# Cross-attention block on one NeuronCore: the first queries and scores in another order, matmuls on the identity ahead of them, the rotary table by a series, weights loaded in pieces

## The chip, the cores and the metric

The kernel runs on one NeuronCore of a Trainium2 chip. The engines named here are TensorE (PE: matmuls and weight loads), VectorE (DVE), ScalarE (ACT), GpSimd (POOL) and SyncE (SP, which issues nearly all DMA transfers). The metric is the device time of one execution in microseconds; the number given for a kernel is the median over its runs.

## The reference

The input is 64 sequences of 32 tokens, 256 wide, and a context of 257 rows of 128 for each sequence. Three residual stages follow each other, each on a layer norm of what stands so far:

1. Cross-attention with 16 heads of 64: queries from the tokens (weights Wq, 256 x 1024), keys and values from the context (Wk, Wv), softmax over 257 context rows, output projection Wo and bias.
2. Self-attention over the 32 tokens of a sequence with 4 heads of 64. Half of each head's width is rotated: `ang[pos, i] = pos * base**(-i/16) * 2*pi/31`, with `base = sigmoid(freq) * c1 + c2` and one input number `freq`; the rotation uses `cos(ang)` and `sin(ang)`.
3. A feed-forward stage with 8 experts, of which each token uses the 2 with the highest router scores.

All is float32.

## The kernel before, in words

Tokens are worked on in 16 tiles of 128 (four sequences each), in the function `block_kernel`. The work has three stretches: a start (constants, loads, the first queries and scores), a loop over 64 sequences in which cross-attention, self-attention and routing of several tiles are interleaved, and the experts' blocks after it.

**Order.** `manual_schedule` (L80) leaves SP and TensorE in the order in which the program writes them. DVE, ACT and POOL are ordered by a planner ahead of the run: it moves an instruction to where it expects the engine to be idle and the inputs to be there, so something written late can stand early in its queue. On the chip each queue is then worked off in that fixed order.

**Loads.** `load` (L98) issues a DMA on SP. In order: `base` (the input number freq, L129), token tiles 0 and 1 (L131), the queries' weights `xwq_sb` (1 MB, L132) and the keys' weights transposed, `xwk_sb` (0.5 MB, L133), the context of tile 0 (L134, two transfers of 0.5 MB), `xwv_sb`, `last_sb`, `xwo_sb`, token tiles 2 and 3 (L139), and the weights of the later stages. After them come eight transfers of zero rows to the DRAM buffer `routed` and one to `out` (L220, L222), from the tile `none`.

**Constants.** POOL makes the identity (L86), zeroes `diag`, `u_ring` and `p_last` (L167, L176, L179) and makes index tables (`iota`, L183).

**Queries.** `cross_queries(c)` (L305) is a generator for two token tiles. Its first step normalises them (`normed`: statistics on DVE, the power -1/2 on POOL at L242, the scaling on DVE at L245). The next transposes them (`transposed`, L248: four transposes on TensorE, two copies on ACT at L253). Then four projections of four heads each (L345, evacuated by ACT at L352) alternate with `of_heads` (L318), which multiplies by the keys' weights (L324) so that scores can be formed on the context itself; its two halves are evacuated by DVE (L337) and ACT (L335). Here `qh` has one buffer, and the PSUM tag `a`, from which `bank` (L231) takes, has three.

**Scores.** `cross_probs(t, b, ..)` (L359) is a generator of four steps for one sequence, each for four heads: scores (L369), maximum on DVE (L373), exp with sum on ACT (L374); after every second one the sums' reciprocal and the scaling on DVE (L379, L381). The scores have three PSUM buffers (tag `s`). `probs_transposed` (L389) and `cross_mix` (L399) use the result one sequence later.

**The start** (L883 to L930): the first step of `cross_queries(0)`; the rotary table, `cos` and `sin`, in the block at L886 to L924 (sigmoid and two sines on ACT, a power of 128 x 16 on POOL, small operations on DVE); all remaining steps of `cross_queries(0)`; the first step of `cross_queries(1)`; then all four steps of `cross_probs(0, 0)`.

**The loop** (L931): for each sequence n it transposes the probabilities, forms the scores of the next sequence, mixes, and takes steps of three generators, "near", "far" and "ahead", as the table `steps` (L875) says. "near" starts as `last_rows` (L259: products with the last context row, stored to DRAM; `load_last`, L296, brings rows of it back) and is `rest(t)` from then on (L597: cross output, self-attention, routing). The rotary table is first read in `self_attention` of tile 0 (L460), which the fifth step of `rest(0)` reaches, in sequence n = 7, the eighth.

Of the kernel before, what the change touches and what calls it, by code (L numbers as in the profile page):

```python
# [9 lines left out]
FP = mybir.dt.float32  # L10
# [40 lines left out]
def block_kernel(  # L51
# [36 lines left out]
    nc.gpsimd.memset(minus_half, -0.5)  # L88
    zero = const.tile([P, 1], FP, name="zero")
    nc.gpsimd.memset(zero, 0.0)  # L90
    half_pi = const.tile([P, 1], FP, name="half_pi")
    nc.gpsimd.memset(half_pi, math.pi / 2)
    expert_id = const.tile([P, NE], FP, name="expert_id")
    nc.gpsimd.iota(
        expert_id, [[1, NE]], base=0, channel_multiplier=0, allow_small_or_imprecise_dtypes=True
# [2 lines left out]
    def load(dst, src):  # L98
        nc.sync.dma_start(out=dst, in_=src)
# [26 lines left out]
        return kvT, kvA  # L126

    base = const.tile([P, 1], FP, name="base")
    load(base, freq.partition_broadcast(P))  # L129
    for t in range(2):  # L130
        load_tokens(t)  # L131
    load(xwq_sb, xwq.rearrange("(c p) k -> p c k", p=P))  # L132
    load(xwk_sb, xwk_t.rearrange("(c p) k -> p c k", p=P))  # L133
    context0 = load_context(0)  # L134
    load(xwv_sb, xwv)
    load(last_sb, ctx_last)
    load(xwo_sb, xwo.rearrange("(c p) k -> p c k", p=P))
    for t in range(2, 4):
        load_tokens(t)  # L139
    load(xbo_bc, xbo.partition_broadcast(P))  # L140

    awqkv_sb = const.tile([P, 2, 3 * D], FP, name="awqkv_sb")
# [18 lines left out]


    routed = tc.dram_tile([NE * CAP, RW], FP, name="routed")

    diag = [const.tile([P, AH, P], FP, name=f"diag{i}") for i in range(2)]
    for d in diag:
        nc.gpsimd.memset(d, 0.0)  # L167

    u_ring = [const.tile([P, D], FP, name=f"u{i}") for i in range(3)]
    p_last = [
        [const.tile([P, 32], FP, name=f"p_last{i}_{b}") for b in range(4)] for i in range(2)
    ]
    for u in u_ring:
        nc.gpsimd.memset(u, 0.0)  # L176
    for ring in p_last:
        for p in ring:
            nc.gpsimd.memset(p, 0.0)  # L179

    def iota(shape, pattern, base, by_partition, name):
        it = const.tile([P] + shape, FP, name=name)
        nc.gpsimd.iota(  # L183
            it,
            pattern,
            base=base,
            channel_multiplier=by_partition,
            allow_small_or_imprecise_dtypes=True,
        )
        return it  # L190

    ones = const.tile([P, P], FP, name="ones")
    nc.gpsimd.memset(ones, 1.0)

    before = iota([P], [[1, P]], 0, -1, "before")
    nc.vector.tensor_scalar(before, before, 0.0, None, ALU.is_gt)
    region = iota([1, NE], [[0, 1], [CAP, NE]], 0, 0, "region")
    expert_id2 = iota([2, NE], [[0, 2], [1, NE]], 0, 0, "expert_id2")

    upto = iota([NE, NE], [[1, NE], [-1, NE]], 0, 0, "upto")  # L200
    nc.vector.tensor_scalar(upto, upto, 0.0, None, ALU.is_ge)

    late = iota([LATE], [[1, LATE]], 0, 0, "late")
    in_lane = iota([LATE // LANES, LANES], [[1, LATE // LANES], [0, LANES]], FAR, 0, "in_lane")
    late_expert = iota([LATE, NE], [[0, LATE], [1, NE]], 0, 0, "late_expert")

    early = iota([EARLY // 2, 2], [[1, EARLY // 2], [EARLY // 2, 2]], 0, 0, "early")
    early_expert = iota([EARLY, NE], [[0, EARLY], [1, NE]], 0, 0, "early_expert")
    row = iota([1], [[0, 1]], 0, 1, "row")
    minus_spare = iota([1], [[0, 1]], -TOK, -1, "minus_spare")  # L210
    token = iota([NT], [[P, NT]], 0, 1, "token")

    seen = const.tile([P, NE], FP, name="seen")
    nc.gpsimd.memset(seen, 0.0)
    xp = pool("xp", 3)
    none = xp.tile([P, RW], FP, tag="xg", bufs=5, name="none")
    nc.gpsimd.memset(none, 0.0)

    for e in range(NE):
        load(routed[e * CAP : e * CAP + P, :], none)  # L220

    load(out[TOK : TOK + P, :], none[:, :D])  # L222

    qp = pool("q", 2)
    pp = pool("p", 2)
    ptp = pool("pt", 2)
    wk = pool("wk", 2)
    sm = pool("sm", 4)
    tb = pool("tb", 1)

    def bank(shape, name):  # L231
# [568 lines left out]
    def late_blocks(done):  # L800
# [67 lines left out]
        )  # L868
        return bl, total

# [12 lines left out]
    work = {"near": last_rows(), "far": iter(()), "ahead": cross_queries(0)}  # L883
    next(work["ahead"])

    with tc.tile_pool(name="rope", bufs=1) as rp:  # L886
        pos = rp.tile([P, 1], FP, name="pos")
        for s in range(P // SEQ):
            nc.gpsimd.iota(
                pos[s * SEQ : (s + 1) * SEQ, :],  # L890
                [[0, 1]],
                base=0,
                channel_multiplier=1,
                allow_small_or_imprecise_dtypes=True,
            )
        expo = rp.tile([P, 16], FP, name="expo")
        nc.gpsimd.iota(
            expo, [[-1, 16]], base=0, channel_multiplier=0, allow_small_or_imprecise_dtypes=True
        )
        expo16 = rp.tile([P, 16], FP, name="expo16")  # L900
        nc.vector.tensor_scalar(expo16, expo, 1.0 / 16.0, None, ALU.mult)
        sig = rp.tile([P, 1], FP, name="sig")
        nc.scalar.activation(sig, base, AF.Sigmoid, bias=zero)
        base2 = rp.tile([P, 1], FP, name="base2")
        nc.vector.tensor_scalar(base2, sig, SDT_L, MIN_L * BASE, ALU.mult, ALU.add)
        base16 = rp.tile([P, 16], FP, name="base16")
        nc.vector.tensor_copy(base16, base2.to_broadcast([P, 16]))
        inv_freq = rp.tile([P, 16], FP, name="inv_freq")
        nc.gpsimd.tensor_tensor(inv_freq, base16, expo16, ALU.pow)
        ang = rp.tile([P, 16], FP, name="ang")  # L910
        nc.vector.tensor_scalar(ang, inv_freq, pos, ANGLE, ALU.mult, ALU.mult)

        s4 = rp.tile([P, 16], FP, name="s4")
        c4 = rp.tile([P, 16], FP, name="c4")
        nc.scalar.activation(s4, ang, AF.Sin, bias=zero, scale=0.25)
        nc.scalar.activation(c4, ang, AF.Sin, bias=half_pi, scale=-0.25)
        s2 = rp.tile([P, 16], FP, name="s2")
        c2 = rp.tile([P, 16], FP, name="c2")
# [203 lines left out]
```

## Time and profile before

| what | value |
|---|---|
| median of 3 runs | 852.11 us (851.6 to 853.08) |
| the profiled execution | 853.89 us, its span 851.9 us |
| TensorE busy | 794.0 us (93% of the span) |
| DVE, ACT, POOL busy | 489.2, 382.3, 147.4 us |
| mean granted TensorE clock | 0.986 |
| DMA | 62.71 MB, mean 74 GB/s |

The span goes from the first to the last instruction of the profiled execution. In the lines shown below, a row of the timeline gives start and duration in microseconds, the engine, the line of the kernel, the operation, the tiles written and read, and in brackets how long the engine was idle before it and what ended this. A float32 matmul appears as two instructions, a transpose as one. L-numbers are lines of the kernel before.

### The profile page before, as it was taken

To read this page: it belongs to the slowest core of one execution; us is meant where nothing else is said; L and a number is where in the kernel's file an instruction comes from. 1 tells how busy PE (TensorE), PEld (TensorE's weight loads), DVE (VectorE), ACT (ScalarE), POOL (GpSimd) and SP (SyncE) were. 2 spreads that over 40 slices of the span, in tenths; PEclk is the share of its full clock that TensorE was granted. 3 is DMA by queue.
4 is the path that set the end of the run, shared out by engine and by line. 5 is a ranking of instruction groups with operands and counts; after the bars stand their busy time and mean duration, and the time that the engine had idled before them with its cause. 6 is when DMAs were issued, how large, how long until landed. Compare 5 with 4: busy or idle time off the path is not lost. (4 is left out here: it accounts for less than half of the span.)

```text
span 851.9 us, 15173 instructions
## 1 busy us (share of the span) xinstructions
PE 794.0 (93%) x5240; PEld 611.9 (72%) x5240; DVE 489.2 (57%) x2006; ACT 382.3 (45%) x1082; POOL 147.4 (17%) x209
## 2 busy tenths in 40 slices
PE   4899999999999999999999999999949999999994
PEld 3567677677767766776766777666647799999993
DVE  2456656766676676667676666767626733333331
ACT  2565545455455445546554545554414332222220
POOL 5001011111101011121101011110112422322222
PEclk9999999999999999999999999999979999999997
DMA  8421102020120202021120202012061297357321
GB/s 300 125 53 53 63 1 72 1 85 19 55 75 11 74 0 86 7 67 37 49 72 2 72 1 72 20 53 55 1 258 13 69 318 216 47 110 221 52 38 22
DMA packets 32031, 62.71 MB, mean 74 GB/s; under 512 B 5256, under 2 KB 22672, under 8 KB 30416
## 3 DMA queue, kind: packets, MB, share of 16 engines
q1 hardware_dynamic: 25424, 52.65, 19.0%
q0 software_dynamic: 6528, 9.06, 6.0%
q8 instruction: 43, 0.70, 0.3%
q14 instruction: 36, 0.29, 0.1%
HBM read 83.23 MB, written 13.16 MB: 113 GB/s over the span
## 5 line engine op out<-in xcount | busy, mean ns | idle before, releaser
L374 ACT ACTIVATE pr<-s,nmx 128x257 f32<-128x257 f32 x256 | 120.8, 479 | 72.6 <-DVE nmx L373 71.4
L369 PE MATMUL s<-kv,q 128*128 128x257 f32 x512 | 143.4, 389 | 7.6 <-ACT pr L374 7.6
L373 DVE TENSOR_REDUCE nmx<-s 128x1 f32<-128x257 f32 x256 | 103.8, 420 | 61.7 <-PE s L369 59.9
L402 PE MATMUL pa<-pt,kv 128*128 128x512 f32 x256 | 123.3, 604 | 5.0 <-ACT ov L426 5.0
L369 PEld LDWEIGHTS s<-kv,q 128*128 128x128 f32 x512 | 88.8, 192 | 25.1 <-ACT pr L374 12.2
L396 ACT COPY pt<-tp 128x512 f32<-128x512 f32 x128 | 75.9, 593 | 65.2 <-PE tp L392 65.1
L392 PEld LDWEIGHTS tp<-ident,pr 128*128 128x128 f32 x512 | 60.7, 144 | 33.7 <-issue 20.9
L392 PE MATMUL tp<-ident,pr 128*128 128x128 f32 x512 | 81.4, 280 | 1.2 <-DVE pr L381 1.1
L381 DVE TENSOR_SCALAR pr<-pr,inv 128x256 f32<-128x256 f32 x256 | 80.5, 357 | 2.9
L405 ACT COPY cT<-pa 128x512 f32<-128x512 f32 x64 | 37.5, 586 | 88.7 <-PE pa L402 88.7
L578 POOL DMA_INDIRECT routed<-xr,rslots x32 | 32.8, 1025 | 250.7 <-DVE pr L381 105.4
L402 PEld LDWEIGHTS pa<-pt,kv 128*128 128x128 f32 x256 | 44.9, 190 | 40.6 <-issue 29.1
L345 PE MATMUL pqh<-xqT,xwq_sb 128*128 128x256 f32 x256 | 62.5, 389 | 4.3 <-ACT xqT L253 4.3
L763 POOL DMA_INDIRECT out_x<-y_late,to_late x28 | 43.4, 1550 | 110.3 <-DVE gate_late L705 41.4
L435 PE MATMUL po<-xwo_sb,ov 128*128 128x256 f32 x256 | 61.9, 386 | 0.0
L345 PEld LDWEIGHTS pqh<-xqT,xwq_sb 128*128 128x128 f32 x256 | 48.6, 195 | 11.6 <-ACT xqT L253 4.7
L435 PEld LDWEIGHTS po<-xwo_sb,ov 128*128 128x128 f32 x256 | 49.7, 194 | 7.1
L379 DVE RECIPROCAL inv<-sums 128x2 f32<-128x2 f32 x128 | 20.6, 161 | 55.9 <-ACT pr L374 55.2
L745 DVE SCALAR_TENSOR_TENSOR g_late<-pb_late,lane,sa_late 128x128 f32<-128x128 f32 x72 | 20.3, 343 | 55.5 <-PE pb_late L726 37.0
L374 ACT ACTIVATION_READ_ACCUMULATOR pr<-s,nmx 128x1 f32 x256 | 51.8, 203 | 0.0
L410 POOL TENSOR_TENSOR xb<-x,xbo_bc 128x256 f32<-128x256 f32 x16 | 11.6, 725 | 213.7 <-issue 198.5
L450 PE MATMUL pqkv<-awqkv_sb,xaT 128*128 128x512 f32 (+1 forms) x128 | 43.9, 486 | 0.0
(256 smaller groups left out, 1286.5 us busy)
## 6 DMA issues: line engine op xcount, KB each, us to landing
lane<-in_wall SPq DMA_DIRECT2D x24, 1028.0 KB
lane<-in_wall SPq DMA_DIRECT2D x24, 512.0 KB
lane2a<-in_wall SPq DMA_DIRECT2D x10, 1028.0 KB
kv<-in_ctx_t SPq DMA_DIRECT2D x16, 514.0 KB
kv<-in_ctx_a SPq DMA_DIRECT2D x16, 512.0 KB
lane2b<-in_wall SPq DMA_DIRECT2D x10, 512.0 KB
xg_late<-routed SPq DMA_DIRECT2D x28, 132.5 KB
x<-in_x SPq DMA_DIRECT2D x16, 128.0 KB
```

The costliest lines, as they stand in the source:

```text
L345: nc.tensor.matmul(pq[:, mm, :], xwq_sb[:, k, m * P : (m + 1) * P], xqT[:, k, :], start=(k == 0), stop=(k == 1),)
L369: nc.tensor.matmul(s, qb[:, g * P : (g + 1) * P], kvT[:, b, :], start=True, stop=True)
L373: nc.vector.tensor_reduce(nmx, s, AX.X, ALU.max, negate=True)
L374: nc.scalar.activation(pr[:, g, :], s, AF.Exp, bias=nmx, accum_out=sums[:, g : g + 1])
L381: nc.vector.tensor_scalar(pr[:, i, :ML], pr[:, i, :ML], inv[:, i : i + 1], None, ALU.mult)
L392: nc.tensor.transpose(tp[:, g * P : (g + 1) * P], pr[:, g, j * P : (j + 1) * P], ident)
L396: nc.scalar.copy(pt, tp)
L402: nc.tensor.matmul(pa, kvA[:, b, j, :], pts[j], start=(j == 0), stop=(j == MC - 1))
L405: nc.scalar.copy(cT[:, :, b, :], pa.rearrange("p (h n) -> p h n", n=SEQ))
L435: nc.tensor.matmul(po, ov[:, m, :], xwo_sb[:, m, :], start=False, stop=(m == XH // 2 - 1))
L450: nc.tensor.matmul(pq, xaT[:, k, :], awqkv_sb[:, k, lo:hi], start=(k == 0), stop=(k == 1))
L763: nc.gpsimd.indirect_dma_start(out=out[:, :], out_offset=bass.IndirectOffsetOnAxis(ap=self.to[:, b : b + 1], axis=0), in_=y, in_offset=Non ...
```

## The change

- The load of `base` leaves the head of the loads and is issued in the loop, at sequence n = 3.
- `xwq_sb` and `xwk_sb` are loaded in four pieces each, alternating; each pair holds what four heads need. Token tiles 2 and 3 are loaded right after the context of tile 0.
- `diag`, `u_ring` and `p_last` are zeroed by DVE in place of POOL, and with the index tables and the zero rows they are written after the first step of `cross_queries(0)`.
- Fifteen matmuls of the identity by the identity are written ahead of all other work of TensorE; nothing reads their result.
- The remaining steps of `cross_queries(0)` and the four steps of `cross_probs(0, 0)` are written interleaved: transposes, projections 0 and 1, heads 0, projection 2, scores 0, heads 1, projection 3, scores 1, heads 2 and 3, scores 2 and 3.
- The rotary table is made in `rotary_tables`, called at n = 5 in the loop: the sigmoid by exp and a reciprocal, one power of 128 x 1 and repeated products for the 16 frequencies, sine and cosine of an eighth of the angle by a series, and three doublings.

```diff
--- before.py
+++ after.py
@@ -88,8 +88,6 @@
     nc.gpsimd.memset(minus_half, -0.5)
     zero = const.tile([P, 1], FP, name="zero")
     nc.gpsimd.memset(zero, 0.0)
-    half_pi = const.tile([P, 1], FP, name="half_pi")
-    nc.gpsimd.memset(half_pi, math.pi / 2)
     expert_id = const.tile([P, NE], FP, name="expert_id")
     nc.gpsimd.iota(
         expert_id, [[1, NE]], base=0, channel_multiplier=0, allow_small_or_imprecise_dtypes=True
@@ -126,17 +124,18 @@
         return kvT, kvA
 
     base = const.tile([P, 1], FP, name="base")
-    load(base, freq.partition_broadcast(P))
     for t in range(2):
         load_tokens(t)
-    load(xwq_sb, xwq.rearrange("(c p) k -> p c k", p=P))
-    load(xwk_sb, xwk_t.rearrange("(c p) k -> p c k", p=P))
+    for i in range(4):
+        w = slice(4 * HD * i, 4 * HD * (i + 1))
+        load(xwq_sb[:, :, w], xwq[:, w].rearrange("(c p) k -> p c k", p=P))
+        load(xwk_sb[:, 2 * i : 2 * i + 2, :], xwk_t[w, :].rearrange("(c p) k -> p c k", p=P))
     context0 = load_context(0)
+    for t in range(2, 4):
+        load_tokens(t)
     load(xwv_sb, xwv)
     load(last_sb, ctx_last)
     load(xwo_sb, xwo.rearrange("(c p) k -> p c k", p=P))
-    for t in range(2, 4):
-        load_tokens(t)
     load(xbo_bc, xbo.partition_broadcast(P))
 
     awqkv_sb = const.tile([P, 2, 3 * D], FP, name="awqkv_sb")
...
-    diag = [const.tile([P, AH, P], FP, name=f"diag{i}") for i in range(2)]
-    for d in diag:
-        nc.gpsimd.memset(d, 0.0)
...
-    for u in u_ring:
-        nc.gpsimd.memset(u, 0.0)
-    for ring in p_last:
-        for p in ring:
-            nc.gpsimd.memset(p, 0.0)
...
-    none = xp.tile([P, RW], FP, tag="xg", bufs=5, name="none")
-    nc.gpsimd.memset(none, 0.0)
-
-    for e in range(NE):
-        load(routed[e * CAP : e * CAP + P, :], none)
-
-    load(out[TOK : TOK + P, :], none[:, :D])
...
+    def rotary_tables():
+
+        with tc.tile_pool(name="rope", bufs=1) as rp:
+            pos = rp.tile([P, 1], FP, name="pos")
...
+
+            sig = rp.tile([P, 1], FP, name="sig")
+            nc.scalar.activation(sig, base, AF.Exp, bias=zero, scale=-1.0)
+            nc.vector.tensor_scalar(sig, sig, 1.0, None, ALU.add)
+            nc.vector.reciprocal(sig, sig)
+            base2 = rp.tile([P, 1], FP, name="base2")
+            nc.vector.tensor_scalar(base2, sig, SDT_L, MIN_L * BASE, ALU.mult, ALU.add)
+
+            part = rp.tile([P, 1], FP, name="part")
+            nc.gpsimd.memset(part, -1.0 / 16.0)
+            root = [rp.tile([P, 1], FP, name=f"root{i}") for i in range(4)]
+            nc.gpsimd.tensor_tensor(root[0], base2, part, ALU.pow)
+            inv_freq = rp.tile([P, 16], FP, name="inv_freq")
+            nc.vector.memset(inv_freq[:, 0:1], 1.0)
+            for i in range(4):
+                n = 1 << i
+                nc.vector.tensor_scalar(
+                    inv_freq[:, n : 2 * n], inv_freq[:, 0:n], root[i], None, ALU.mult
+                )
+                if i < 3:
+                    nc.vector.tensor_tensor(root[i + 1], root[i], root[i], ALU.mult)
+
+            def of_16(name):
+                return rp.tile([P, 16], FP, name=name)
+
+
+            t8, sq, s8, c8 = of_16("t8"), of_16("sq"), of_16("s8"), of_16("c8")
+            nc.vector.tensor_scalar(t8, inv_freq, pos, ANGLE / 8, ALU.mult, ALU.mult)
+            nc.vector.tensor_tensor(sq, t8, t8, ALU.mult)
+
+            def series(acc, highest):
+                nc.vector.tensor_scalar(acc, sq, term(highest), None, ALU.mult)
+                for n in range(highest - 2, 1, -2):
+                    nc.vector.scalar_tensor_tensor(acc, acc, term(n), sq, ALU.add, ALU.mult)
+
+            def term(n):
+                return (-1.0) ** (n // 2) / math.factorial(n)
+
+            series(s8, 11)
+            nc.vector.scalar_tensor_tensor(s8, s8, 1.0, t8, ALU.add, ALU.mult)
+            series(c8, 10)
+            nc.vector.tensor_scalar(c8, c8, 1.0, None, ALU.add)
+
+            def doubled(s1, c1, s2, c2, name):
+                nc.vector.scalar_tensor_tensor(s2, s1, 2.0, c1, ALU.mult, ALU.mult)
+                square = of_16(name)
+                nc.vector.tensor_tensor(square, s1, s1, ALU.mult)
+                nc.vector.tensor_scalar(c2, square, -2.0, 1.0, ALU.mult, ALU.add)
+
+            s4, c4, s2, c2 = of_16("s4"), of_16("c4"), of_16("s2"), of_16("c2")
+            doubled(s8, c8, s4, c4, "square8")
+            doubled(s4, c4, s2, c2, "square4")
+            doubled(s2, c2, sin[:, 0, :], cos[:, 0, :], "square2")
+
...
     work = {"near": last_rows(), "far": iter(()), "ahead": cross_queries(0)}
     next(work["ahead"])
...
+    diag = [const.tile([P, AH, P], FP, name=f"diag{i}") for i in range(2)]
+    for d in diag:
+        nc.vector.memset(d, 0.0)
...
+    for u in u_ring:
+        nc.vector.memset(u, 0.0)
+    for ring in p_last:
+        for p in ring:
+            nc.vector.memset(p, 0.0)
...
-    with tc.tile_pool(name="rope", bufs=1) as rp:
...
-        nc.vector.tensor_scalar(expo16, expo, 1.0 / 16.0, None, ALU.mult)
-        nc.scalar.activation(sig, base, AF.Sigmoid, bias=zero)
-        nc.vector.tensor_scalar(base2, sig, SDT_L, MIN_L * BASE, ALU.mult, ALU.add)
-        nc.vector.tensor_copy(base16, base2.to_broadcast([P, 16]))
-        nc.gpsimd.tensor_tensor(inv_freq, base16, expo16, ALU.pow)
-        nc.vector.tensor_scalar(ang, inv_freq, pos, ANGLE, ALU.mult, ALU.mult)
-        nc.scalar.activation(s4, ang, AF.Sin, bias=zero, scale=0.25)
-        nc.scalar.activation(c4, ang, AF.Sin, bias=half_pi, scale=-0.25)
-        nc.vector.scalar_tensor_tensor(s2, s4, 2.0, c4, ALU.mult, ALU.mult)
-        nc.vector.tensor_mul(c2, s4, s4)
-        nc.vector.tensor_scalar(c2, c2, -2.0, 1.0, ALU.mult, ALU.add)
-        nc.vector.scalar_tensor_tensor(sin[:, 0, :], s2, 2.0, c2, ALU.mult, ALU.mult)
-        nc.vector.tensor_mul(s4, s2, s2)
-        nc.vector.tensor_scalar(cos[:, 0, :], s4, -2.0, 1.0, ALU.mult, ALU.add)
...
+    none = xp.tile([P, RW], FP, tag="xg", bufs=5, name="none")
+    nc.gpsimd.memset(none, 0.0)
+    for e in range(NE):
+        load(routed[e * CAP : e * CAP + P, :], none)
+    load(out[TOK : TOK + P, :], none[:, :D])
+    warm = bank([P], "warm")
+    for _ in range(15):
+        nc.tensor.matmul(warm, ident, ident, start=True, stop=True)
+    scores = cross_probs(0, 0, kvs[0][0])
+    for i in range(5):
+        next(work["ahead"])
+    next(scores)
+    for i in range(2):
+        next(work["ahead"])
+    next(scores)
     for _ in work["ahead"]:
+        pass
+    for _ in scores:
         pass
     work["ahead"] = cross_queries(1)
     next(work["ahead"])
-    for _ in cross_probs(0, 0, kvs[0][0]):
-        pass
     for n, (t, b) in enumerate(seqs):
+        if n == 3:
+            load(base, freq.partition_broadcast(P))
+        if n == 5:
+            rotary_tables()
         if t == NT - 1 and b == 0:
             blocks, done = early_blocks()
             lane_of_queries(0)
```

More of the change, by code (lines that the diff above doesn't have):

```diff
@@ L163, in block_kernel @@
     routed = tc.dram_tile([NE * CAP, RW], FP, name="routed")
-    diag = [const.tile([P, AH, P], FP, name=f"diag{i}") for i in range(2)]
-    for d in diag:
-        nc.gpsimd.memset(d, 0.0)
[L171 to L174, printed above, removed]
-    for u in u_ring:
-        nc.gpsimd.memset(u, 0.0)
-    for ring in p_last:
-        for p in ring:
-            nc.gpsimd.memset(p, 0.0)
[L181 to L215, printed above, removed]
-    none = xp.tile([P, RW], FP, tag="xg", bufs=5, name="none")
-    nc.gpsimd.memset(none, 0.0)
-    for e in range(NE):
-        load(routed[e * CAP : e * CAP + P, :], none)
-    load(out[TOK : TOK + P, :], none[:, :D])
     qp = pool("q", 2)
@@ L228, in block_kernel @@
     sm = pool("sm", 4)
+    xp = pool("xp", 3)
     tb = pool("tb", 1)
@@ L869, in late_blocks @@
         return bl, total
+    def rotary_tables():
+        with tc.tile_pool(name="rope", bufs=1) as rp:
+            pos = rp.tile([P, 1], FP, name="pos")
+            for s in range(P // SEQ):
+                nc.gpsimd.iota(
+                    pos[s * SEQ : (s + 1) * SEQ, :],
+                    [[0, 1]],
+                    base=0,
+                    channel_multiplier=1,
+                    allow_small_or_imprecise_dtypes=True,
+                )
[15 more added lines that the diff above has]
+                    inv_freq[:, n : 2 * n], inv_freq[:, 0:n], root[i], None, ALU.mult
+                )
+                if i < 3:
[24 more added lines that the diff above has]
+            doubled(s2, c2, sin[:, 0, :], cos[:, 0, :], "square2")
@@ L884, in block_kernel @@
     next(work["ahead"])
-    with tc.tile_pool(name="rope", bufs=1) as rp:
[L887 to L896, printed above, removed]
-        nc.gpsimd.iota(
-            expo, [[-1, 16]], base=0, channel_multiplier=0, allow_small_or_imprecise_dtypes=True
-        )
-        expo16 = rp.tile([P, 16], FP, name="expo16")
-        nc.vector.tensor_scalar(expo16, expo, 1.0 / 16.0, None, ALU.mult)
-        sig = rp.tile([P, 1], FP, name="sig")
-        nc.scalar.activation(sig, base, AF.Sigmoid, bias=zero)
-        base2 = rp.tile([P, 1], FP, name="base2")
-        nc.vector.tensor_scalar(base2, sig, SDT_L, MIN_L * BASE, ALU.mult, ALU.add)
-        base16 = rp.tile([P, 16], FP, name="base16")
-        nc.vector.tensor_copy(base16, base2.to_broadcast([P, 16]))
[L908 to L915, printed above, removed]
-        nc.scalar.activation(c4, ang, AF.Sin, bias=half_pi, scale=-0.25)
-        s2 = rp.tile([P, 16], FP, name="s2")
-        c2 = rp.tile([P, 16], FP, name="c2")
-        nc.vector.scalar_tensor_tensor(s2, s4, 2.0, c4, ALU.mult, ALU.mult)
-        nc.vector.tensor_mul(c2, s4, s4)
-        nc.vector.tensor_scalar(c2, c2, -2.0, 1.0, ALU.mult, ALU.add)
-        nc.vector.scalar_tensor_tensor(sin[:, 0, :], s2, 2.0, c2, ALU.mult, ALU.mult)
-        nc.vector.tensor_mul(s4, s2, s2)
-        nc.vector.tensor_scalar(cos[:, 0, :], s4, -2.0, 1.0, ALU.mult, ALU.add)
@@ new lines, in block_kernel, with iota @@
+    diag = [const.tile([P, AH, P], FP, name=f"diag{i}") for i in range(2)]
+    for d in diag:
+        nc.vector.memset(d, 0.0)
+    u_ring = [const.tile([P, D], FP, name=f"u{i}") for i in range(3)]
+    p_last = [
+        [const.tile([P, 32], FP, name=f"p_last{i}_{b}") for b in range(4)] for i in range(2)
+    ]
+    for u in u_ring:
[3 more added lines that the diff above has]
+            nc.vector.memset(p, 0.0)
+    def iota(shape, pattern, base, by_partition, name):
+        it = const.tile([P] + shape, FP, name=name)
+        nc.gpsimd.iota(
+            it,
+            pattern,
+            base=base,
+            channel_multiplier=by_partition,
+            allow_small_or_imprecise_dtypes=True,
+        )
+        return it
@@ new lines, in block_kernel @@
+    ones = const.tile([P, P], FP, name="ones")
+    nc.gpsimd.memset(ones, 1.0)
+    before = iota([P], [[1, P]], 0, -1, "before")
+    nc.vector.tensor_scalar(before, before, 0.0, None, ALU.is_gt)
+    region = iota([1, NE], [[0, 1], [CAP, NE]], 0, 0, "region")
+    expert_id2 = iota([2, NE], [[0, 2], [1, NE]], 0, 0, "expert_id2")
+    upto = iota([NE, NE], [[1, NE], [-1, NE]], 0, 0, "upto")
+    nc.vector.tensor_scalar(upto, upto, 0.0, None, ALU.is_ge)
+    late = iota([LATE], [[1, LATE]], 0, 0, "late")
@@ new lines, in block_kernel @@
+    in_lane = iota([LATE // LANES, LANES], [[1, LATE // LANES], [0, LANES]], FAR, 0, "in_lane")
+    late_expert = iota([LATE, NE], [[0, LATE], [1, NE]], 0, 0, "late_expert")
+    early = iota([EARLY // 2, 2], [[1, EARLY // 2], [EARLY // 2, 2]], 0, 0, "early")
+    early_expert = iota([EARLY, NE], [[0, EARLY], [1, NE]], 0, 0, "early_expert")
+    row = iota([1], [[0, 1]], 0, 1, "row")
+    minus_spare = iota([1], [[0, 1]], -TOK, -1, "minus_spare")
+    token = iota([NT], [[P, NT]], 0, 1, "token")
@@ new lines, in block_kernel @@
+    seen = const.tile([P, NE], FP, name="seen")
+    nc.gpsimd.memset(seen, 0.0)
+    none = xp.tile([P, RW], FP, tag="xg", bufs=5, name="none")
[9 more added lines that the diff above has]
+        next(work["ahead"])
```

## The prediction

> **What bounds the kernel now.** I read first the page's engine totals and slices, to see which engine bounds and where it is not full; then a table of windows over the start; then the instructions of the first 34 us in order of time.
>
> ```profile
> span 851.9 us, 15173 instructions
> PE 794.0 (93%) x5240; PEld 611.9 (72%) x5240; DVE 489.2 (57%) x2006; ACT 382.3 (45%) x1082; POOL 147.4 (17%) x209
> ...
> PE   4899999999999999999999999999949999999994
> ```
>
> TensorE is busy 794.0 of 851.9 us. The slices say where the other 58 us lie: half of the first one, some of the second, one near 620 us, the last. The change touches only the first two (and one place in the first tile after them), so its gain can be no more than what is idle or slow there.
>
> ```profile
> 0.00:30.00 30.00, 16.92 (x74) 11.89 (x74) 10.08 (x35) 9.65 (x16) 12.94 (x52) 1.00 0.81 268
> 30.16:33.57 3.41, 1.51 (x5) 0.71 (x5) 2.10 (x9) 2.15 (x9) 0.00 (x0) 1.00 0.82 281
> 33.57:36.98 3.41, 3.41 (x12) 2.79 (x12) 1.07 (x4) 1.82 (x6) 0.00 (x0) 0.50 0.03 8
> 37.00:60.00 23.00, 23.00 (x140) 16.39 (x139) 12.18 (x40) 14.73 (x42) 0.00 (x0) 1.00 0.21 50
> ```
>
> The columns after the window are its length, then the busy time of PE, weight loads, DVE, ACT and POOL, then the granted clock, the DMA share and GB/s. To 30 us TensorE works 16.92 us. From 37 us on it never stops (23.00 of 23.00): from there everything is queued behind TensorE, and what the start gives is kept. In between stands a stretch at clock 0.50: after 3.4 us in which TensorE was 44% busy (1.51 of 3.41) it ran 3.4 us at half speed.
>
> ```profile
> 7.27 1.22 PE L252 MATMUL trq<-ident,xnq 128*128 128x128 f32 x4 [7.27 <-DVE xnq L245]
> 8.48 2.91 POOL L909 TENSOR_TENSOR inv_freq<-base,expo 128x16 f32<-128x16 f32 x1
> 11.70 0.31 ACT L915 ACTIVATE s<-ang,zero 128x16 f32<-128x16 f32 x1 [5.30 <-DVE ang L911]
> 12.11 0.62 ACT L253 COPY xqT<-trq 128x256 f32<-128x256 f32 x2
> 12.78 5.54 PE L345 MATMUL pqh<-xqT,xwq_sb 128*128 128x256 f32 x16 [4.29 <-ACT xqT L253]
> 22.32 1.13 PE L324 MATMUL pq<-qh,xwk_sb 64*128 64x256 f32 x8 [1.00 <-DVE q L337]
> 28.98 1.28 ACT L374 ACT_TABLE_LOAD   x1
> 30.89 0.70 PE L369 MATMUL s<-kv,q 128*128 128x257 f32 x2 [1.06 <-ACT pr L374]
> 33.39 0.71 PE L392 MATMUL tp<-ident,pr 128*128 128x128 f32 x2 [0.36 <-DVE pr L381]
> 33.90 1.92 PE L369 MATMUL s<-kv,q 128*128 128x257 f32 x4
> ```
>
> Each row: start, duration, engine, line, what it writes and reads; in brackets the idle time before and who ended it. The transposes of the normalised tokens end at 8.49, but ScalarE copies them only at 12.11: in its queue stand the sines ahead of the copy, and these wait for POOL's power of 2.91 us. Then the first 16 projection matmuls take 5.54 us, where the later eights take 1.99. Until about 16.2 they come 0.43 us apart, after it 0.22 to 0.25: half speed, though the clock column shows 1.00 there (it knows no state before the first change). After that come queries, then all of the first softmax with nothing beside it. The point that I measure to is 33.90: the next sequence's scores start, and the steady loop begins.
>
> **The change, part by part.**
>
> *Rotary table out of the way of the copy.* Sigmoid, two sines, two table loads, ten DVE operations and the wide power leave the start. The copies then follow the transposes at once: 4.29 us of wait are open.
>
> *Warm-up.* Fifteen matmuls on the identity, two instructions each (L369 shows two for one), stand ahead of the transposes in TensorE's hand-written order. The identity is ready at 1.48 us. At full clock such 128x128 by 128 instructions come 0.11 us apart (L726: 16 in 1.78 us from start to start of the next group), at half 0.22. With the gate opening some 4 us after the start, as it did 3.4 us after 12.78, it is 18 x 0.22 + 12 x 0.11 = 5.3 us: end at 6.9. That is a wait that the change adds: the transposes are queued behind it. They could not start much sooner: the tokens, loaded first now (one 0.46 us issue earlier than 3.80), are normalised by about 6 us. Transposes 0.6 at full clock, a copy of 0.37 and hand-overs: first projection at 8.2 instead of 12.78, **-4.6 us**. A gate that opens at once gives 7.3, one that opens two microseconds later 9.0.
>
> *Weights in pieces, more DMA issues.* Eight issues in place of two on SP, 6 x 0.45 = 2.7 us more ahead of the context. The first piece pair ends at 0.65 MB of the stream. The window from 0 to 5 us has a mean of 124 GB/s, 0.62 MB, which puts that near 5 us; x of tile 2 landed 3 us after its place in the stream, so 5 to 8 us: just in time. The context's first half ends at 2.36 MB (251 GB/s over the first 10 us), so 10 to 12.5 us; it is wanted at about 14.6. Nothing waits, but by 1 to 2 us only for the first piece. The zero rows and the next tile's loads stand behind the same queue as before, with over 20 us to spare.
>
> *Interleaving.* From the first projection I lay out TensorE's new order with warm pitches from the rows: projection pair 1.73 (8 x 0.216), heads 1.07, score group 0.43, 0.33 at each return from 64 to 128 rows. Four projections 6.9, four heads 4.3, four scores 1.7, three returns 1.0; a wait of 1.0 before the last heads (PSUM bank, as at 22.32), 0.5 for the last copies; then from the last score group to 33.90's counterpart 3.0 as from 30.89 to 33.90, of which 0.4 is counted. Sum 18.0 us. The softmax of the first two groups now lies under projections; the exp table load (1.28) is no longer between scores and exp. DVE may still be put behind the wait for tokens 2 and 3, as in before where it stood 6.13 us for them to 19.13; their loads come earlier now, so I add 1.0. 19.0 against 33.90 - 12.78 = 21.1: **-2.1 us**.
>
> *The table load, by row and by rule.* In before the load took 1.28 us, and exp started at 30.28, right behind it, where its input was ready at 29.44: a cost of 0.84. The Trainium skill (ScalarE: Activation LUTs, "What ACT_TABLE_LOAD costs") adds a drain of about 1.38, 2.66 us in all for a switch; the row shows none. If the load now falls ahead of the first copy, it costs 0 to 1.3 us by the row and up to 2.7 by the rule. ScalarE is idle to 7 us, so I take 0.
>
> *The gate.* The stretch at half clock cost up to 3.4 x 0.5 = 1.7 us. The Trainium skill (TensorE: Matmul & The Clock Gate, Part 1) closes the gate after an idle window of about 3.4 us; by that rule the new order, with no gap above 2 us, keeps it open. The row speaks against this: 44% busy was enough to close it, and the new order still has a stretch around its last two score groups of 40 to 60%. I take it as staying open, for **-1.5 us**; closing again costs that back.
>
> *Memsets and index tables.* 2 x 0.52, 3 x 0.31 and 8 x 0.12 us, 3.0 us by POOL's rows, go to DVE, which is idle until 3.80 and from 13 to 19. Counted at nothing; without the cover they would delay a query copy by up to 3. POOL's tables now follow the normalisation's power; the zero rows wait for them until long before SP comes to them (21.77).
>
> *Rotary by series.* 34 DVE operations of 0.17 at a pitch of 0.20 (dependent chain at L623 to L627) are 6.8 us, one power of 0.55, one exp. They fall into the first two tiles, where DVE is 53% (37 to 60) to 61% busy. The planner moves ready work into idle slots, as POOL's L855 at 8.25 shows, and the tables are not wanted before the eighth sequence. Between 0 (all in gaps) and 3.8 (one block, less some 3 us that three score buffers and one sequence of lead cover), I take **+0.6**.
>
> Sum: -4.6 - 2.1 - 1.5 + 0.6 = -7.6. The profiled execution took 853.89 us, 2.0 more than its span, and 1.8 more than the median: 846.3 there, and on the median 852.11 - 7.6 = **844.5 us**. A change under 0.2% (1.7 us) can't be told from none here.
>
> **The rivals.**
>
> *The gate closes again.* For it: 44% busy closed it before. Then 1.5 is lost, 846.0; with a late warm-up too, 847.
>
> *The series stands as a block on DVE.* For it: the operations are written ahead of the sixth sequence's own; against it the gaps named above. +3.8 in place of +0.6: 847.7.
>
> *Data late instead of ScalarE late.* The first piece or a query copy behind tokens 2 and 3 takes the place of the wait removed: half of the 4.6 plus 2.1 gone, 848.
>
> *The gain is given back* at a later wait, such as TensorE's 9.74 us for u near 620: 852. Against it: that wait hangs on DMAs which themselves follow TensorE's work, so it moves along.
>
> *Slower.* The base frequency's load now stands on SP behind the stores of the last rows, where SP once waited 19.6 us. ScalarE takes its queue in order: if exp(base) is planned earlier than the load lands, all exps and evacuations stand. It decides from about 12 us (7.6 + 1.7, and some 3 covered); with 14 it gives 855. The largest such misplacement in before is 6.13 us.
>
> **How the numbers follow.** Forecast 0.60 (844.5, own range 842.5 to 846.5), gate 0.15, block 0.12, late data 0.05, given back 0.03, slower 0.05. Faster by over 0.2% are the first four, 0.92; same 0.03; slower 0.05. The low end 841.9 adds an early gate (-0.9), no rotary cost (-0.6) and no DVE wait (-1.0); the high end 848.6 takes in most of the block and of late data. About 0.17 is left out.
>
> **What would show it.** First projection near 8.2, its sixteen instructions in about 3.8 us; the counterpart of 33.90 near 27.2 or before; clock 1.00 through it; TensorE as full as before from there to 60 us after, with the series' rows scattered between DVE's reductions. The prediction is wrong if projections wait for weights, if exp(base) or the series shows waiting reductions around it, or if the gain at the loop's start is not found at the end.

## The result, and the profile after

The changed kernel takes 847.55 us in the median (845.95 to 850.82), the kernel before on the same chip 851.64 us (850.7 to 853.81): a ratio of 0.9953 [0.9942, 0.9965], so 4.1 us or 0.47% faster. The direction is as forecast and the time lies in the range, but the size is little more than half of the 7.6 us that the sum gave. The profiled execution took 847.14 us.

The page's totals and two rows of its slices, after:

```profile
span 845.4 us, 15266 instructions
PE 796.3 (94%) x5270; PEld 615.3 (73%) x5270; DVE 494.6 (59%) x2043; ACT 379.1 (45%) x1078; POOL 142.7 (17%) x195
...
PE   8999999999999999999999999999859999999994
PEclk9999999999999999999999999999979999999998
```

The first slice of TensorE went from 4 to 8 and the second from 8 to 9, but the 8 holds 30 instructions that nothing reads: TensorE's busy time grew by 2.3 us (794.0 to 796.3). A fuller slice is no gain by itself. The timeline of the start, after (start, duration, engine, line, tiles, idle time before; from here on L-numbers are lines of the kernel that ran):

```profile
0.74 1.28 ACT L193 ACT_TABLE_LOAD   x1 [0.74 <-PEq L1152]
1.51 6.47 PE L955 MATMUL warm<-ident 128*128 128x128 f32 x30 [1.51 <-POOL ident masks.py:199]
4.97 0.99 DVE L185 TENSOR_SCALAR xnq<-x,mvq,rstdq 128x256 f32<-128x256 f32 x2 [0.32 <-POOL rstdq L182]
8.94 3.72 PE L285 MATMUL pqh<-xqT,xwq_sb 128*128 128x256 f32 x16 [0.52 <-ACT xqT L193]
12.59 1.13 PE L264 MATMUL pq<-qh,xwk_sb 64*128 64x256 f32 x8
13.66 0.43 DVE L177 BATCH_NORM_STATS2 stq<-x 128x6 f32<-128x256 f32 x1 [5.57 <-DMA x<-in_x]
15.34 0.93 DVE L185 TENSOR_SCALAR xnq<-x,mvq,rstdq 128x256 f32<-128x256 f32 x2 [0.32 <-POOL rstdq L182]
16.18 0.68 DVE L277 COPY q<-pq 128x512 f32<-128x512 f32 x1
16.96 0.67 PE L309 MATMUL s<-kv,q 128*128 128x257 f32 x2 [1.32 <-ACT qh L292]
...
27.53 1.03 PE L309 MATMUL s<-kv,q 128*128 128x257 f32 x4
```

The table of activations is loaded at 0.74, in ScalarE's idle time, and the first projection starts at 8.94 instead of 12.78. The first heads' product (L264) ends at 13.72. Its copy out of PSUM by DVE (L277), which the first scores need, starts only at 16.18: ahead of it in DVE's queue stands the normalisation of token tiles 2 and 3, which are needed much later, and DVE stood 5.57 us until tile 2 had landed at 13.66. The bracket of the scores names ScalarE's `qh`, but that ended at 16.28; the copy ended at 16.86, 0.1 us ahead of them. The same two rows in before, where the product ended at 19.39:

```profile
19.13 0.43 DVE L237 BATCH_NORM_STATS2 stq<-x 128x6 f32<-128x256 f32 x1 [6.13 <-DMA x<-in_x]
...
21.59 0.68 DVE L337 COPY q<-pq 128x512 f32<-128x512 f32 x1
```

Landing to copy is 2.46 us in before and 2.52 in after. So the start has two chains that meet in this copy: tokens 0 and 1, transposes, projection and heads on the one side, the landing of tokens 2 and 3 on the other. In the first trace of before they end 2.2 us apart.

### The profile page after: what moved, and what is told of

Same layout as the page of the kernel before. It is cut to its first block, busy times and chain, and to the rows that moved or that the text cites. A ratio compares the mean times of both kernels' runs of the same rounds, so it can differ in the third digit from the quotient of the medians.

```text
span 845.4 us, 15266 instructions
## 1 busy us (share of the span) xinstructions
PE 796.3 (94%) x5270; PEld 615.3 (73%) x5270; DVE 494.6 (59%) x2043; ACT 379.1 (45%) x1078; POOL 142.7 (17%) x195
## 5 line engine op out<-in xcount | busy, mean ns | idle before, releaser
L345 ACT COPY cT<-pa 128x512 f32<-128x512 f32 x64 | 37.5, 586 | 88.4 <-PE pa L342 88.4
L285 PE MATMUL pqh<-xqT,xwq_sb 128*128 128x256 f32 x256 | 60.7, 380 | 0.5 <-ACT xqT L193 0.5
```

The costliest lines, as they stand in the source:

```text
L285: nc.tensor.matmul(pq[:, mm, :], xwq_sb[:, k, m * P : (m + 1) * P], xqT[:, k, :], start=(k == 0), stop=(k == 1),)
```

## Experiments

Ratios are to the kernel before, timed beside each of them on the same chip, with a 95% interval. What theory A and theory B stand for differs from run to run; each expectation says it. "Gate" is short for TensorE's clock being at half speed (closed) or full speed (open), as the clock column shows it.

**The kernel before once more**, for what differs between two executions. No edit.

> The kernel before, once more. My theory: the profiled executions differ by 6.5 us and the medians by 4.1 because the profiled execution of before was one of its long ones; the stretch at half clock (33.6 to 37.0 us) is in some executions only. Then the spans of its runs spread over 1.5 us or more, and another trace may show clock 1.00 there, with a span near 849.9. Rival: the stretch is in every execution; then this trace shows it again and the missing 2.4 us lie in the changed kernel.

851.46 us, ratio 0.9996 [0.9987, 1.0005]. Windows over the end of the start, first of the recorded trace of before, then of this one (length, busy PE, weight loads, DVE, ACT, POOL, clock, DMA share, GB/s):

```profile
33.57:36.98 3.41, 3.41 (x12) 2.79 (x12) 1.07 (x4) 1.82 (x6) 0.00 (x0) 0.50 0.03 8
```

```profile
33.50:37.00 3.50, 3.50 (x30) 3.35 (x28) 2.30 (x9) 2.97 (x11) 0.00 (x0) 1.00 0.03 7
```

The half-clock stretch, 12 matmul instructions in 3.4 us where the other execution did 30 in 3.5, is in one execution and not in the other. Here tokens 2 landed at 17.56 instead of 19.13, and the next sequence's scores started at 32.61 instead of 33.90. The span was 848.3 instead of 851.9 us. Two executions of one kernel thus differ by nearly as much as the change brings, and a trace can't be subtracted from a trace without asking which of the two is the usual one.

**Without the warm-up.**

```diff
-    warm = bank([P], "warm")
-    for _ in range(15):
-        nc.tensor.matmul(warm, ident, ident, start=True, stop=True)
```

> The changed kernel without the fifteen matmuls on the identity. They ran 6.47 us, all at half speed, and the transposes stood behind them to 7.82. Theory A (the warm-up buys little): transposes near 5.5 to 6.5, first projection near 7.5 at half speed for 3.4 us, so the first 16 take 5.4 in place of 3.7 and end within 0.5 us of the changed kernel's 12.6; time within 0.8 us of it. Theory B (it is worth what it was counted at): 1.5 us or more slower, or projections wait for weights so that the early start is worth nothing.

848.42 us, 0.9944 [0.9931, 0.9958]: the time of the whole change. The transposes start at 5.04 instead of 7.82 and the first projection at 6.76 instead of 8.94; its sixteen instructions then take 5.03 us instead of 3.72, the first six of them at half speed. What the warm-up wins in clock it spends in waiting. Nothing of either reaches the scores:

```profile
6.76 5.03 PE L285 MATMUL pqh<-xqT,xwq_sb 128*128 128x256 f32 x16 [0.46 <-ACT xqT L193]
11.73 1.13 PE L264 MATMUL pq<-qh,xwk_sb 64*128 64x256 f32 x8
12.79 1.99 PE L285 MATMUL pqh<-xqT,xwq_sb 128*128 128x256 f32 x8
17.57 0.67 PE L309 MATMUL s<-kv,q 128*128 128x257 f32 x2 [2.79 <-issue]
```

The heads end at 12.86, tokens 2 land at 13.64, the copy starts at 16.78, and the first scores follow it after TensorE was idle for 2.79 us.

**Without the interleaving**: the remaining steps of the first queries are written before all scores, as in before.

```diff
     scores = cross_probs(0, 0, kvs[0][0])
-    for i in range(5):
-        next(work["ahead"])
-    next(scores)
-    for i in range(2):
-        next(work["ahead"])
-    next(scores)
     for _ in work["ahead"]:
```

> The changed kernel with all scores after all queries, all else kept. Theory A (as predicted, the interleaving is worth about 2 us): the next sequence's scores start 1 to 2.5 us later than 27.5, and the time is 1 to 2.5 us longer. If the gate closes again after this longer stretch, another 1.7. Theory B: the wait of VectorE for tokens 2 and 3 hits the interleaved order alone (1.3 us), so that both orders come out within 0.5 us.

847.28 us, 0.9942 [0.9928, 0.9955]. From the first projection to the next sequence's scores it is 19.35 us (7.76 to 27.11), with the interleaving 18.59 (8.94 to 27.53). So it gives at most 0.8 us in the trace and nothing that the times show: with scores first or heads first, TensorE waits for the same copy.

**The rotary table alone**: before, with the load of `base` and the series placed as in after, and nothing else.

```diff
-    load(base, freq.partition_broadcast(P))
...
-    with tc.tile_pool(name="rope", bufs=1) as rp:
...
     for n, (t, b) in enumerate(seqs):
+        if n == 3:
+            load(base, freq.partition_broadcast(P))
+        if n == 5:
+            rotary_tables()
```

> The kernel before with only the rotary table moved: its input loaded at the fourth sequence, the series at the sixth. Theory A: copies follow the transposes at once, first projection near 9.2 in place of 12.8, -3.6 us at the start; the series costs 1.7 us in the loop (as from 7.88 to 6.14 us of lead in the changed kernel); net 1.9 us faster than before. Theory B: the lead is filled by waits for weights (1 MB in one piece); then under 0.5 us or slower.

852.78 us, 1.0006 [0.9997, 1.0015]: nothing. The number lies near B's, but not for B's cause. No projection waits for weights; the first one starts at 8.96, 3.8 us earlier than before. DVE waits longer in exchange:

```profile
16.12 0.43 DVE L236 BATCH_NORM_STATS2 stq<-x 128x6 f32<-128x256 f32 x1 [8.37 <-DMA x<-in_x]
...
20.05 0.68 DVE L336 COPY q<-pq 128x512 f32<-128x512 f32 x1
20.79 1.77 PE L323 MATMUL pq<-qh,xwk_sb 64*128 64x256 f32 x8 [2.50 <-DVE q L336]
```

The heads were done at 16.38, their copy came at 20.05. TensorE stood 2.50 us for it and did the next eight products in 1.77 instead of 1.13 us, at clock 0.50 (21.15 to 24.56). Against the 3.8 us stand 0.8 in the first projections (6.35 us instead of 5.54), 1.5 in the longer wait for the copy and 1.7 in the half-clock stretch; the exp's table load, now at 0.74 and no longer between scores and exp, gives 0.9 back. The next scores start at 33.10, between the two traces of before (33.90 and 32.61), and the series in the loop costs 1.74 us more (shown below).

**The loads of tokens 2 and 3 put back**, in the changed kernel.

```diff
     context0 = load_context(0)
-    for t in range(2, 4):
-        load_tokens(t)
     load(xwv_sb, xwv)
     load(last_sb, ctx_last)
     load(xwo_sb, xwo.rearrange("(c p) k -> p c k", p=P))
+    for t in range(2, 4):
+        load_tokens(t)
```

> The changed kernel with tokens 2 and 3 loaded again behind the output weights, as in the kernel before; all else kept. In each trace so far VectorE's first query copy stands 2.5 us behind the landing of tokens 2 (13.66 and 16.18 in the changed kernel, 17.56 and 20.02 in the second trace of before). Theory A (this landing, not ScalarE's late copy, sets the start): tokens 2 land near 17.5 to 18.5, the copy ends near 20.5 to 21.5, the second sequence's scores start 4 us later than 27.5, and most of the gain is gone: 850 to 852. Theory B (the table's move, the warm-up and the interleaving carry the gain): within 1 us of the changed kernel.

855.23 us, 1.0039 [1.0026, 1.0052]: slower than the kernel before, where theory A still had a little of the gain left (850 to 852). Everything else of the change is in it. Against the change's 0.9953 the place of these two loads is worth 7.3 us by the ratios, and the next scores come 7.16 us later (34.69 and 27.53). The tokens land at 17.50, the copy starts at 21.43:

```profile
17.50 0.43 DVE L177 BATCH_NORM_STATS2 stq<-x 128x6 f32<-128x256 f32 x1 [9.74 <-DMA x<-in_x]
...
21.43 0.68 DVE L277 COPY q<-pq 128x512 f32<-128x512 f32 x1
22.21 1.20 PE L309 MATMUL s<-kv,q 128*128 128x257 f32 x2 [7.40 <-issue]
```

TensorE stands 7.40 us, and the clock is 0.50 in the window from 20 to 24 and 0.62 from 24 to 27.

**These two loads alone** in the kernel before, and then **the table and these two loads** there, without warm-up, interleaving, pieces or moved memsets.

```diff
     context0 = load_context(0)
+    for t in range(2, 4):
+        load_tokens(t)
     load(xwv_sb, xwv)
     load(last_sb, ctx_last)
     load(xwo_sb, xwo.rearrange("(c p) k -> p c k", p=P))
-    for t in range(2, 4):
-        load_tokens(t)
```

> The kernel before with only the loads of tokens 2 and 3 moved ahead of the values' weights. Theory A (the landing of tokens 2 counts only once the table is out of the way): they land near 13.5 and the first query copy is no longer held, but the first projection stays at 12.8; that frees the 1.0 us wait before the second heads and little more: 0.7 to 1.5 us faster than before. Theory B (the load order alone carries the change): 3.5 us or more faster.

> The kernel before with two parts of the change: the table moved into the loop, and tokens 2 and 3 loaded ahead of the values' weights. No warm-up, no pieces, no interleaving. Theory A (these two, neither of which brings much alone, are the change): first projection near 9.0 at half speed, first copy at 16 with no wait, the second sequence's scores near 28; 3 to 5 us faster than before, within 1.2 us of the changed kernel. Theory B (warm-up, pieces or interleaving add to it): 2 us or more slower than the changed kernel.

Alone 850.89 us, 0.9985 [0.9977, 0.9992], some 1.3 us. With the table 847.92 us, 0.9954 [0.9941, 0.9967]: the whole change, as far as the times can tell (in the trace the next scores come 1.0 us later than in the changed kernel, 28.53 and 27.53).

```profile
11.65 0.43 DVE L236 BATCH_NORM_STATS2 stq<-x 128x6 f32<-128x256 f32 x1 [3.90 <-DMA x<-in_x]
...
14.87 1.14 PE L323 MATMUL pq<-qh,xwk_sb 64*128 64x256 f32 x8
16.03 0.69 DVE L336 COPY q<-pq 128x512 f32<-128x512 f32 x1 [1.15 <-PE pq L323]
```

DVE now waits for TensorE, and no longer TensorE for DVE. With the tokens in time and the table still ahead of the copies, TensorE is the late one (the heads end at 20.54, the tokens landed at 13.95); with the table gone and the tokens late, DVE is. Only both together let the first copy start earlier, at 16.03, right after its heads.

**Tokens 2 and 3 loaded ahead of the context**, in the changed kernel.

```diff
-    context0 = load_context(0)
     for t in range(2, 4):
         load_tokens(t)
+    context0 = load_context(0)
```

> The changed kernel with tokens 2 and 3 loaded ahead of the context of tile 0 (1 MB less before them). Theory A: they land near 11, VectorE is through with them at 13.5, just as the first heads are there; TensorE's wait of 1.3 us before the first scores goes, and the time is 1 to 1.5 us shorter. Theory B: the context now lands too late or the wait comes back at the next copy; within 0.5 us.

845.17 us, 0.9923 [0.991, 0.9936]. They land at 10.12, and the first scores no longer wait for DVE: the copy starts at 13.02, its heads having ended at 12.99.

**The weights in one load each**, in the changed kernel.

```diff
-    for i in range(4):
-        w = slice(4 * HD * i, 4 * HD * (i + 1))
-        load(xwq_sb[:, :, w], xwq[:, w].rearrange("(c p) k -> p c k", p=P))
-        load(xwk_sb[:, 2 * i : 2 * i + 2, :], xwk_t[w, :].rearrange("(c p) k -> p c k", p=P))
+    load(xwq_sb, xwq.rearrange("(c p) k -> p c k", p=P))
+    load(xwk_sb, xwk_t.rearrange("(c p) k -> p c k", p=P))
```

> The changed kernel with the queries' and the keys' weights in one load each. Theory A (the pieces count only where projections would start before the whole 1 MB is there): the whole has its place at 1.3 MB of the stream, near 7.5 to 9 us, and projections start at 8 to 9; at most 1 us later, time within 1 us. Theory B (pieces carry part of the gain): projections start near 10.5, 1.5 us or more slower.

845.81 us, 0.9927 [0.9913, 0.9941], against 0.9953 with the pieces. The first projection starts at 8.40 and waits for no weights. SP comes to tokens 2 at 4.32 instead of 7.01, and they land at 12.13 instead of 13.66:

```profile
12.13 0.43 DVE L175 BATCH_NORM_STATS2 stq<-x 128x6 f32<-128x256 f32 x1 [4.31 <-DMA x<-in_x]
...
14.66 0.68 DVE L275 COPY q<-pq 128x512 f32<-128x512 f32 x1
```

The copy again comes 2.53 us after the landing. The pieces push this landing, so in the changed kernel they cost 1.5 us in the trace (next scores at 27.53 and 26.02) and 2.2 by the ratios.

**The series at the start**, in the changed kernel; first with the load of `base` after the weights, then with it first and the tokens ahead of the context, then with the tokens after the third pair of pieces.

```diff
+    load(base, freq.partition_broadcast(P))   # after the weights; in the other two ahead of all
...
     next(work["ahead"])
+    rotary_tables()
...
-        if n == 3:
-            load(base, freq.partition_broadcast(P))
-        if n == 5:
-            rotary_tables()
```

> The changed kernel with the series in VectorE's idle time of the start (its input loaded ahead of the context), nothing of it in the loop. Theory A (the series costs 1.7 us in the loop): the lead over before is the same at the second sequence and at the first cross output, -1.7 us; but 20 of its operations now stand behind tokens 2 and ahead of the first query copy, which costs some 1.5 at the start. Net within 0.7 us of the changed kernel, with the loss moved from 50 us to 16 us. Theory B (the 1.7 us are not the series'): the loss near 50 us stays, and the kernel is 1.5 us slower.

> Tokens 2 and 3 ahead of the context and the series at the start with its input loaded first of all. Theory A (both losses are VectorE's queue): the query copy near 15.5, no loss near 50 us: 1.5 to 2.5 us shorter than the changed kernel. Theory B: one of the two losses is paid in another place; within 0.7 us.

> As the kernel with both losses taken out (series at the start with its input first, tokens 2 and 3 ahead of the context), but tokens 2 and 3 one piece pair earlier. There the first scores waited 0.89 us for the query copy. Theory A: the tokens land near 9.8, the wait goes to 0.3 or less, 0.3 to 0.9 us shorter than it. Theory B: the series, not the landing, now holds the copy; no difference (within 0.5).

The first, 850.19 us, 0.9975 [0.9968, 0.9982], loses what it should have kept. Its exp of `base` was planned ahead of the first copies on ScalarE, the load landed at 11.1, and the whole start stood behind it:

```profile
11.11 1.28 ACT L826 ACT_TABLE_LOAD   x1 [11.11 <-DMA base<-in_freq]
12.61 0.62 ACT L194 COPY xqT<-trq 128x256 f32<-128x256 f32 x2
13.29 5.71 PE L286 MATMUL pqh<-xqT,xwq_sb 128*128 128x256 f32 x16 [5.07 <-ACT xqT L194]
```

Neither theory of this run had that; it is the mechanism of the prediction's slower rival, in another place. With `base` first it is there at 3.65, and ScalarE has its copies done in time: 844.67 us, 0.9908 [0.9894, 0.9922], and with the tokens a little earlier still 844.01 us, 0.9902 [0.9887, 0.9918]. In the former the series still holds the copy (14.86, its heads having ended at 12.82), in the latter nothing does. Their times can't be told apart, and both beat the changed kernel by about 4 us.

What the series costs in the loop shows in windows from one instruction (the products L219, in before L279) to another (the products L358, in before L418) of the first two tiles: the changed kernel, then the last experiment.

```profile
34.18:61.53 27.35, 25.75 (x146) 17.63 (x145) 17.76 (x79) 17.51 (x50) 0.55 (x1) 1.00 0.30 82
```

```profile
32.73:58.34 25.61, 25.61 (x146) 17.66 (x145) 14.49 (x46) 17.54 (x49) 0.00 (x0) 1.00 0.31 87
```

The same 146 matmul instructions take 27.35 us with the series among them and 25.61 without it, as in before and in the other runs with the series elsewhere: 1.74 us. Where, the timeline after shows:

```profile
53.46 0.60 PE L309 MATMUL s<-kv,q 128*128 128x257 f32 x2
...
55.76 0.18 DVE L870 TENSOR_SCALAR cos<-square 128x16 f32<-128x16 f32 x1
55.85 0.42 DVE L313 TENSOR_REDUCE nmx<-s 128x1 f32<-128x257 f32 x1
...
57.60 0.56 PE L332 MATMUL tp<-ident,pr 128*128 128x128 f32 x2 [1.60 <-DVE pr L321]
```

The last thirteen operations of the series (54.52 to 55.85) stand in one piece ahead of a reduction. In before it started 0.64 us after its scores, here 2.39, and TensorE stands 1.60 us for the probabilities that follow. The same two rows in before:

```profile
61.34 0.60 PE L369 MATMUL s<-kv,q 128*128 128x257 f32 x2
...
61.98 0.43 DVE L373 TENSOR_REDUCE nmx<-s 128x1 f32<-128x257 f32 x1 [1.01 <-PE s L369]
```

The two chains, over all traces, in us: end of the first heads, start of DVE's statistics of tile 2, start of the first copy, next sequence's scores.

| kernel | heads end | tokens 2 | copy | next scores | ratio |
|---|---|---|---|---|---|
| before | 19.39 | 19.13 | 21.59 | 33.90 | |
| before again | 19.27 | 17.56 | 20.02 | 32.61 | 0.9996 |
| table alone | 16.38 | 16.12 | 20.05 | 33.10 | 1.0006 |
| tokens alone | 20.54 | 13.95 | 20.58 | 33.98 | 0.9985 |
| table and tokens | 16.01 | 11.65 | 16.03 | 28.53 | 0.9954 |
| the change | 13.72 | 13.66 | 16.18 | 27.53 | 0.9953 |
| tokens put back | 12.89 | 17.50 | 21.43 | 34.69 | 1.0039 |
| no warm-up | 12.86 | 13.64 | 16.78 | 28.14 | 0.9944 |
| not interleaved | 12.54 | 13.18 | 15.71 | 27.11 | 0.9942 |
| series at start | 20.06 | 15.54 | 20.09 | 32.31 | 0.9975 |
| whole weights | 13.18 | 12.13 | 14.66 | 26.02 | 0.9927 |
| tokens ahead of context | 12.99 | 10.12 | 13.02 | 25.26 | 0.9923 |
| series and `base` at start, tokens ahead | 12.82 | 10.84 | 14.86 | 26.26 | 0.9908 |
| the same, tokens earlier | 13.78 | 9.14 | 13.81 | 26.09 | 0.9902 |

Where the copy is not within 0.04 us of the heads' end, it is 2.5 to 4.0 us behind the tokens; in the last row but one the series fills that time.

## Why the prediction was right and wrong

The changed kernel's start came out nearly as forecast: the next scores at 27.53, where the terms gave 12.78 - 4.6 + 19.0 = 27.2. The gain did not, and 847.55 lies outside the forecast's own range (842.5 to 846.5), at the figures of the rivals (846 to 848). From the 7.6 us to about the 3.3 that the traces show behind the series, the terms are: 1.3 because the start of before was taken from a trace whose next scores came at 33.90 and not at 32.61, 1.5 for the gate, 1.1 for the series, 0.3 for the start after. Of the signs that it named, the sixteen instructions (3.72 us) and the clock of 1.00 came; a sign against it came too, a reduction waiting beside the series.

**The first step's credit** is what failed in the mechanism. It gave the 4.6 us to the table and the warm-up, and left DVE's wait for tokens 2 and 3 as 1.0 us inside the interleaving; the move of their loads got no line of its own. The first projection did come earlier, at 8.94 where 8.2 was forecast (the transposes came at 7.82, where the warm-up was to end at 6.9: all thirty instructions ran at half speed). But the table alone brought nothing, and the change without the earlier loads is slower than before. The gain is that of two moves together. The rival "data late instead of ScalarE late" named just this wait and priced it at 848; it was given a chance of 0.05. The row with DVE's 6.13 us for tokens 2 lay open in the trace of before, its copy 2.46 us behind. What was not done is to ask which end comes last once the other chain is shorter by 4.

**Interleaving** from the first projection took 18.6 us where 19.0 was forecast. But the forecast took its -2.1 from 21.1 us, a trace with the late tokens in it. Against the other trace of before (19.83) it is -1.2, and in the changed kernel the old order costs 0.8 in the trace and nothing in the times.

**The gate** (-1.5) was taken from one execution. The change keeps it open in its trace, as forecast, but so did the kernel before in its second trace. Before's profiled execution, 853.89 us, lay 2.2 above the median of 851.64. The mean clock of every execution says more. Of the 27 of before timed beside its repetition, 12 had 0.987 or less and a median of 852.95 us, 15 had 0.988 or more and 851.28; one stretch of 3.41 us at half speed is just this step of 0.002 and 1.7 us. Of the changed kernel's 14, 5 had 0.987 or less (848.57), 9 more (847.13). So the size of the term was right where the stretch falls, but before has such a stretch in fewer than half of its executions and the change hardly more seldom: some 0.15 us on average, an estimate from these counts. (The mean doesn't tell where the stretch lies; the trace without the warm-up has its longer one near 614 us.) That the change's trace kept the gate open was luck, as the last section shows.

**The series** cost 1.74 and not 0.6. The mechanism was a block after all, but of thirteen operations and not of all 34, so its price is below the rival's 3.8.

**Pieces** were counted as hiding. They hide from the projections, as forecast, but they delay the tokens behind them in the queue, and DVE stood for those: 1.5 to 2 us. That the forecast looked for a waiting weight and not for the load behind it is the same omission as in the first step.

**At nothing**, and rightly: the table load at 0.74, before any copy, and the wait for u near 620, which is 9.6 us where it was 9.7 and gave nothing back.

With these sizes the sum becomes, against the trace of before without the half-clock stretch: first projection -3.8, from there to the next scores -1.2, series +1.7, together -3.3 where the medians differ by 4.1. The remaining 0.8 is not made by half-clock stretches: the executions with a clock of 0.988 or more differ by 4.2 (851.28 and 847.13). The two traces show that something late adds to it. By the copy `cT` of each sequence (L405 in before, L345 after) the lead is 5.08 us at the first sequence, 3.34 at the fifth, 3.32 at the 61st, 4.17 at the last, and 2.95 at the end of the span: 0.85 is won near 600 us and 1.2 lost in the experts' blocks. Neither was followed to its cause. Left open too: what warm-up and interleaving would bring where the tokens are early. Their removal was tried only with the copy waiting for tokens, which covers either.

## What to carry to other kernels

When an instruction is made ready earlier, look in the queue of the engine that takes its result for what stands ahead of it: a load that is wanted much later can hold the urgent copy, and then the load's place is the thing to move. Undo the parts of a change singly and in pairs, since two parts that are worth nothing alone can carry all of it. Take no more than a share of a term that only one execution showed.

## What the hardware showed beside this

The granted clock changes only at the borders of windows of 3.41 us. All stretches of one clock that begin and end within the fourteen traces are whole multiples of it (3.41, 6.83, 13.65, 17.07 and more), and where the borders lie differs from trace to trace. Counted from a trace's own changes, the share in which TensorE was busy in one window tells the clock of the next. Of the 3346 windows at full clock in these traces, all that were less than 47% busy were followed by half clock and all from 52.8% on by full clock; of the two between, 47.5% was followed by full and 52.5% by half clock. Two windows at this edge, of the run with the series at the start and the tokens ahead of the context, and of the change:

```profile
22.73:26.14 3.41, 1.79 (x8) 0.95 (x9) 2.03 (x8) 1.66 (x5) 0.00 (x0) 1.00 0.78 252
26.14:29.55 3.41, 3.41 (x11) 2.78 (x12) 0.95 (x3) 2.02 (x6) 0.00 (x0) 0.50 0.84 197
```

```profile
24.60:28.01 3.41, 1.80 (x9) 1.31 (x10) 1.92 (x7) 1.41 (x5) 0.00 (x0) 1.00 0.80 208
28.01:31.42 3.41, 3.41 (x27) 3.15 (x26) 2.30 (x7) 3.10 (x12) 0.00 (x0) 1.00 0.95 298
```

Busy for 1.79 us it closed, for 1.80 us it stayed open; the ends of matmuls are modelled, so the edge is known to a few per cent only. In both runs the same gap of 1.58 us stands before the probabilities' transposes. In the run with the tokens earlier still a border at 24.73 cuts that gap in two, the windows are 79% and 72% busy, and the clock stays. The Trainium skill (TensorE: Matmul & The Clock Gate, Part 1) closes the gate after an idle window of about 3.4 us; here the window need not be idle: in the starts of these traces windows that were 27, 32, 44, 46 and 53% busy closed it.

It opens in the same way. In the eight traces with the warm-up ahead of everything the first change to full speed came at 5.07 to 7.66 us, each time at the end of a window in which TensorE was busy throughout, and so the same thirty instructions took 5.30 to 6.54 us. Since the borders lie elsewhere in each execution, a gate term in a sum needs both ends.
